# Layer 0's attention in batches of 3, 3 and 2 steps, with bounds sums as accumulator outputs

## The chip, the cores and the metric

The kernel runs on one core of a Trainium2 chip. A core has TensorE (matrix products, PE in the profile, with its weight loads as PEld), VectorE (DVE), ScalarE (ACT), GpSimd (POOL), and DMA queues, of which SyncE (SP) issues most here. The engines run side by side and wait for each other through semaphores. Matrix products land in PSUM, eight banks of 128 rows of 512 fp32 values each; everything else lies in SBUF. The metric is the time of one execution on the device in microseconds (us), the median of several.

## The reference

Eight images of 512 channels and 32x32 = 1024 positions pass through four layers. The change lies in layer 0, attention with 8 heads of 64 channels, and in a check of its own that the kernel makes.

```python
h = group_norm(x, gn_scale, gn_bias)
qkv = einsum('oc,bchw->bohw', qkv_w, h) + qkv_b
q, k, v = split(qkv, 3, axis=1)          # then split into 8 heads of 64
attn = softmax(einsum('bnsd,bntd->bnst', q, k) * 64 ** -0.5, axis=-1)
h = einsum('bnst,bntd->bnsd', attn, v)
for _ in range(3):                       # on h as (positions, channels)
    h = h + 0.1 * tanh(h @ inl_w.T + inl_b)
return x + einsum('oc,bchw->bohw', proj_w, h) + proj_b
# layer 1: attention with one head of 64; layer 2: up-sampling, leaky ReLU,
# down-sampling; layer 3: three convolutions with mixed expert weights
```

## The kernel before

P is 128, S 1024, HALF 512, C 512, CC = C/P = 4, SC = S/P = 8, HD 64, B 8. All values are fp32. Exponentials are taken without subtracting a maximum. So that this is safe, the kernel keeps running sums of all exponential totals and their inverses in `seen`, and at the end counts how many of them are within a bound (1e20); where one is not, the whole computation is done again with a maximum subtracted. With the given inputs this second run is not taken.

The pools that matter: `ps_sc` has two buffers of two PSUM banks, `ps_tp` two of one bank, `ps_mm` two of one bank.

```python
def tmp(name, n=HALF):
    if n == HALF:
        return work.tile([P, n], F32, tag="half", name=name, bufs=2)
    return work.tile([P, n], F32, tag="tmp", name=name, bufs=5)

def sums(name):
    return work.tile([P, S], F32, tag="sums", name=name, bufs=2)
```

Attention of one image is done in 8 groups: a pair of heads (`oc`) and a half of the positions (`sh`). A group has 8 steps (`jc`), one for each 128 keys. A step computes scores for both heads of the pair, which use 64 rows of TensorE each and run side by side, then the exponential, a running sum over steps, and the product with the values. At a group's end the sums over the 128 rows are formed by a product with ones (`total`), inverted and multiplied in.

```python
groups = [(oc, sh) for sh in range(2) for oc in range(CC)]
exps, accs, avs = {}, {}, {}

def scores(t):
    g, jc = divmod(t, SC)
    oc, sh = groups[g]
    ps = ps_sc.tile([P, S], F32, tag="scores", name=f"scores_{b}_{t}")
    scores_T(                                     # two matmuls, L266
        [ps[:, ts(r, HALF)] for r in range(2)],
        [k[rows[r], oc, ts(jc, P)] for r in range(2)],
        [q[rows[r], oc, ts(sh, HALF)] for r in range(2)],
        # ... (shifts, only in the second run)
    )
    e = tmp(f"e_{b}_{t}", S)
    nc.scalar.activation(e, ps, AF.Exp, scale=HD ** -0.5)            # L612
    exps[t] = e
    if jc == 1:
        accs[g] = sums(f"acc_{b}_{g}")
        nc.vector.tensor_add(accs[g], exps[t - 1], e)                # L616
    elif jc > 1:
        nc.vector.tensor_add(accs[g], accs[g], e)                    # L618

def weighted(t):
    g, jc = divmod(t, SC)
    oc, sh = groups[g]
    e = exps.pop(t)
    if jc == 0:
        avs[g] = bank(name=f"av_{b}_{g}")                            # ps_mm
    for r in range(2):
        nc.tensor.matmul(                                            # L627
            avs[g][rows[r]], v[:, jc, ts(2 * oc + r, HD)], e[:, ts(r, HALF)],
            start=(jc == 0), stop=(jc == SC - 1),
        )

def normalised(g):
    oc, sh = groups[g]
    acc = accs.pop(g)
    ps = bank(ps_tp, f"total_{b}_{g}")
    for r in range(2):
        nc.tensor.matmul(                                            # L637
            ps[rows[r]], ones[:, 0:HD], acc[:, ts(r, HALF)], start=True, stop=True
        )
    inv = tmp(f"inv_{b}_{g}", HALF)
    nc.vector.reciprocal(inv, ps)                                    # L641
    nc.vector.tensor_mul(hf[:, oc, ts(sh, HALF)], avs.pop(g), inv)   # L642
    for part in (acc[:, 0:HALF], acc[:, HALF:S], inv):
        nc.gpsimd.tensor_add(seen, seen, part)                       # L644

n = len(groups) * SC
for t in range(0, n + 4, 2):
    for u in (t, t + 1):
        if u < n:
            scores(u)
    for u in (t - 2, t - 1):
        if 0 <= u < n:
            weighted(u)
    if t >= SC + 2 and (t - 2) % SC == 0:
        normalised((t - 2) // SC - 1)
```

After attention come three steps with tanh and the projection. Each is a fast matrix product of seven parts over halves of its operands (P1, C11, U2, ...). `quarter_sums` prepares differences of quarters of `hf` on VectorE (L378 to L381; for the first step they are written over `v`). P1 and C11 need only the first half of the positions; C11 adds into the bank of P1 after ScalarE has copied P1 out:

```python
if what == "P1":
    nc.scalar.copy(keep["P1"][u], ps)                                # L514
elif what == "C11":
    tanh(keep["C11"][u], ps, u)                                      # L508
    step(keep["C11"][u], u, 0)                                       # L505
elif what in ("U2", "U3"):
    nc.vector.tensor_add(keep[what][u], ps, keep["P1"][u])
# ...
order = (
    ("P1", "A", "A11", b11), ("C11", "A", "A12", b21), ("U2", "X", "S2", 1),
    # ... the number is the quarter sum that a part needs; the letter its banks
)
```

The check, near the end of the kernel, beside layer 2 of the last image:

```python
def out_of_bounds():
    within = tmp("within")
    nc.vector.tensor_scalar(within, seen, BOUND, None, ALU.is_le)
    count = small.tile([P, 1], F32, tag="count", name="count")
    nc.vector.tensor_reduce(count, within, AX.X, ALU.add)
    ps = bank(ps_tp, "within")
    nc.tensor.matmul(ps[0:1, 0:1], count, ones[:, 0:1], start=True, stop=True)
    # ... compared with P * HALF - 0.5, read into a register
```

The instructions' order on an engine is not always that of the source: the framework orders them when it builds the program, and adds the waits.

Of the kernel before, what the change touches and what calls it, by code (L numbers as in the profile page):

```python
# [9 lines left out]
F32 = mybir.dt.float32  # L10
BF16 = mybir.dt.bfloat16
AF = mybir.ActivationFunctionType
ALU = mybir.AluOpType
AX = mybir.AxisListType
# [3 lines left out]
P = 128  # L18
B, C, H, W = 8, 512, 32, 32
S = H * W  # L20
CC = C // P
SC = S // P
HALF = 512
NH = 8
HD = C // NH
# [16 lines left out]
BOUND = 1e20  # L42
# [11 lines left out]
def tile_sequence(ctx: ExitStack, tc: tile.TileContext, a: dict, out: bass.AP, shifted: bool):  # L54
    nc = tc.nc
    run = "s" if shifted else "u"

    const = ctx.enter_context(tc.tile_pool(name=f"const_{run}", bufs=1))
    big = ctx.enter_context(tc.tile_pool(name=f"big_{run}", bufs=7))
    work = ctx.enter_context(tc.tile_pool(name=f"work_{run}", bufs=2))  # L60
    small = ctx.enter_context(tc.tile_pool(name=f"small_{run}", bufs=4))
    spill = ctx.enter_context(tc.tile_pool(name=f"spill_{run}", bufs=1, space=DRAM))
    ps_sc = ctx.enter_context(tc.tile_pool(name=f"ps_sc_{run}", bufs=2, space=PSUM))
    ps_tp = ctx.enter_context(tc.tile_pool(name=f"ps_tp_{run}", bufs=2, space=PSUM))
# [5 lines left out]
    def bank(pool=None, name="mm"):  # L70
        pool = pool or ps_mm
        return pool.tile([P, HALF], F32, tag="bank", name=name)

    def tmp(name, n=HALF):
        if n == HALF:
            return work.tile([P, n], F32, tag="half", name=name, bufs=2)
        return work.tile([P, n], F32, tag="tmp", name=name, bufs=5)

    def sums(name):
        return work.tile([P, S], F32, tag="sums", name=name, bufs=2)  # L80
# [28 lines left out]

    seen = const.tile([P, HALF], F32, name="seen")  # L110
    nc.vector.memset(seen, 0.0)

    v_row = const.tile([P, C], F32, name="v_row")
    nc.gpsimd.dma_start(v_row, a["v_b"].partition_broadcast(P))
# [191 lines left out]
    def group_norm(b, x, mul, add):  # L306
        h = big_tile(f"h_{b}", [P, CC, S])
        for cc in range(CC):
            nc.vector.tensor_scalar(
                h[:, cc, :], x[:, cc, :], mul[:, cc : cc + 1], add[:, cc : cc + 1],  # L310
                ALU.mult, ALU.add,
            )
        return h
# [39 lines left out]
    def weight_sums(key, t, a21, a22, held=None):  # L353
        if held is not None:

            nc.gpsimd.tensor_copy(t[:, 3, 0, 0:1], held)
        nc.gpsimd.tensor_add(t[:, 3], a21, a22)
        nc.gpsimd.tensor_sub(t[:, 4], t[:, 3], t[:, 0])
        nc.gpsimd.tensor_sub(t[:, 5], t[:, 0], a21)
        nc.gpsimd.tensor_sub(t[:, 6], t[:, 1], t[:, 4])  # L360
        nc.gpsimd.tensor_scalar(t[:, 2], a22, -1.0, None, ALU.mult)
        nc.gpsimd.dma_start(stored[key], t)
        return t
# [202 lines left out]
    def layer0(b, x, norm, w):  # L566
        h = group_norm(b, x, *norm)
        t = quarter_sums(f"h_{b}", h)
        if b == 0:
            for key in "kv":  # L570
                w[key] = weight_sums(key, *held[key], t[3][1][:, 0:1])
        q = big_tile(f"q_{b}", [P, CC, S])
        k = big_tile(f"k_{b}", [P, CC, S])
        v = big_tile(f"v_{b}", [P, SC, C])
        all_of(product(f"q_{b}", w["q"], h, t, channels(f"q_{b}", q, qkv_b[:, 0:CC])))
        w["inl"] = weight("inl", b)
        all_of(product(f"k_{b}", w["k"], h, t, channels(f"k_{b}", k, qkv_b[:, CC : 2 * CC])))
        w["proj"] = weight("proj", b)
        all_of(product(f"v_{b}", w["v"], h, t, positions(f"v_{b}", v, v_row), rows=True))
        w["v1"] = weight("v1", b)  # L580
        hf = big_tile(f"hf_{b}", [P, CC, S])
        rows = [slice(HD * r, HD * r + HD) for r in range(2)]
        shifts = None
        if shifted:
            shifts = big_tile(f"shifts_{b}", [P, CC, S])
            for oc in range(CC):
                for r in range(2):
                    row_shifts(
                        f"{b}_{oc}_{r}", [q[rows[r], oc, :]] * 2,
                        [k[rows[r], oc, ts(h, HALF)] for h in range(2)],  # L590
                        [shifts[HD * r : HD * r + 1, oc, :]],
                    )

        groups = [(oc, sh) for sh in range(2) for oc in range(CC)]
        exps, accs, avs = {}, {}, {}

        def scores(t):
            g, jc = divmod(t, SC)  # L600
            oc, sh = groups[g]
            ps = ps_sc.tile([P, S], F32, tag="scores", name=f"scores_{b}_{t}")
            scores_T(
                [ps[:, ts(r, HALF)] for r in range(2)],
                [k[rows[r], oc, ts(jc, P)] for r in range(2)],
                [q[rows[r], oc, ts(sh, HALF)] for r in range(2)],
                shifts and [
                    shifts[HD * r : HD * r + 1, oc, ts(sh, HALF)] for r in range(2)
                ],
            )  # L610
            e = tmp(f"e_{b}_{t}", S)
            nc.scalar.activation(e, ps, AF.Exp, scale=HD ** -0.5)  # L612
            exps[t] = e
            if jc == 1:
                accs[g] = sums(f"acc_{b}_{g}")
                nc.vector.tensor_add(accs[g], exps[t - 1], e)  # L616
            elif jc > 1:
                nc.vector.tensor_add(accs[g], accs[g], e)  # L618

        def weighted(t):  # L620
            g, jc = divmod(t, SC)
# [3 lines that stand above are left out]
                avs[g] = bank(name=f"av_{b}_{g}")  # L625
# [14 lines that stand above are left out]
            inv = tmp(f"inv_{b}_{g}", HALF)  # L640
            nc.vector.reciprocal(inv, ps)  # L641
            nc.vector.tensor_mul(hf[:, oc, ts(sh, HALF)], avs.pop(g), inv)  # L642
            for part in (acc[:, 0:HALF], acc[:, HALF:S], inv):
                nc.gpsimd.tensor_add(seen, seen, part)  # L644

        n = len(groups) * SC
        for t in range(0, n + 4, 2):
            for u in (t, t + 1):
                if u < n:
                    scores(u)  # L650
            for u in (t - 2, t - 1):
                if 0 <= u < n:
                    weighted(u)
            if t >= SC + 2 and (t - 2) % SC == 0:
                normalised((t - 2) // SC - 1)

        for it in range(3):
            t = quarter_sums(f"hf_{b}_{it}", hf, None if it else v)
            name = f"inl_{b}_{it}"

            banks = None if it else [bank(p, f"{name}_A{u}") for u, p in enumerate((ps_mm, ps_tp))]
            all_of(product(name, w["inl"], hf, t, inner_step(name, hf), first_banks=banks))
        if b + 1 < B:
            w["q"] = weight("q", b + 1)
        t = quarter_sums(f"hf_{b}_3", hf)
        all_of(product(f"proj_{b}", w["proj"], hf, t, residual(f"proj_{b}", x)))
        if b + 1 < B:
            w["k"] = weight("k", b + 1)
# [366 lines left out]
    for i in (1, 2, 3):  # L1035
        g, be, m, v = (load_const(f"{c}{i}", pool3) for c in "gbmv")
# [45 lines left out]
    for i in range(2):  # L1082
        t = pool3.tile([P, H + 2, W + 2], F32, tag=f"rim_{i}", bufs=1, name=f"rim_{i}")
# [17 lines left out]
    def out_of_bounds():  # L1101


        within = tmp("within")
        nc.vector.tensor_scalar(within, seen, BOUND, None, ALU.is_le)
        count = small.tile([P, 1], F32, tag="count", name="count")
        nc.vector.tensor_reduce(count, within, AX.X, ALU.add)
        ps = bank(ps_tp, "within")
        nc.tensor.matmul(ps[0:1, 0:1], count, ones[:, 0:1], start=True, stop=True)
        redo = small.tile([P, 1], mybir.dt.int32, tag="redo", name="redo")  # L1110
        nc.vector.tensor_scalar(redo[0:1, :], ps[0:1, 0:1], P * HALF - 0.5, None, ALU.is_lt)
        return nc.values_load(redo[0:1, 0:1], min_val=0, max_val=1)

    z3 = {}
# [13 lines left out]
    redo = None if shifted else out_of_bounds()  # L1128
    wt_next = mixed(0)
    route(B - 1, B)  # L1130
    for b in range(B):
# [5 lines left out]
        for g in range(2):  # L1137
            ps = bank(name=f"c1_{b}_{g}")
# [21 lines left out]
        for oc in range(CC):  # L1160
            at = C + 9 * P + oc * P
            ps = ps_sc.tile([P, S], F32, tag="scores", name=f"c3_{b}_{oc}")
# [5 lines left out]
            n = S if b + 1 < B else HALF  # L1168
# [75 lines left out]
```

## Time and profile before

| What | Value |
|---|---|
| Time, median of 3 runs | 3939.58 us (3938.11 to 3940.49) |
| Profiled span | 3934.4 us |
| Busy: PE, DVE, ACT, POOL | 98%, 66%, 28%, 11% |
| Attention scores, L266 | 2048 matmul instructions, 511.0 us busy |
| Weighted values, L627 | 2048 matmul instructions, 494.1 us busy |
| Exponentials, L612 | 512 instructions of 128x1024, mean 1021 ns |
| One attention group in mid-image | 16.00 us: PE busy 16.00, DVE 12.75, ACT 7.75, POOL 5.55 |

Reading it: an fp32 matmul shows as two instructions, so a step's two products are four instructions in each of L266 and L627. Busy time is the union of an engine's instructions; the mean of one matmul is longer than its share, because neighbours overlap. The chain of the work that ended last follows the span back from its end: at each step to whatever released the instruction, or to the one before it on its engine. Time of an engine that does not stand on this chain costs nothing by itself.

### The profile page before, as it was taken

Reading aid. Unit: us, or ns where it says so; the run is one execution under the profiler, and the core shown is the slowest. Engines: PE = TensorE matmul, PEld = TensorE weight load, DVE = VectorE, ACT = ScalarE, POOL = GpSimd, SP = SyncE. Lnnn points to the kernel's source line nnn. Section 1 sums busy time; section 2 is a strip of 40 time slices with the busy share of each in tenths; the row PEclk is TensorE's granted clock in tenths of the full one; section 3 lists DMA queues with packets and bytes.
Section 4 is the critical chain, followed back from the end, with each engine's and each line's share of the span. In section 5 each row is a group of like instructions: output and inputs, shape, how many; then the busy total and the mean of one; then the engine's idle time right before and its main releaser. Section 6 shows DMA issues by size and latency. Waiting matters only on the chain.

```text
span 3934.4 us, 37957 instructions
## 1 busy us (share of the span) xinstructions
PE 3868.2 (98%) x14630; PEld 2032.6 (52%) x14630; DVE 2593.8 (66%) x3690; ACT 1105.0 (28%) x1507; POOL 436.1 (11%) x310
## 2 busy tenths in 40 slices
PE   8999999999999999999999999999999999999998
PEld 4336653476435763366434754357534764346543
DVE  4777848764686647775586646765487655766786
ACT  1421224212332114212241123322142122421333
POOL 5310003000120003100030002200031001301000
PEclk9999999999999999999999999999999999999999
DMA  5002310122101310023101221013200131003432
GB/s 197 19 0 83 115 57 1 40 77 100 38 0 59 118 68 11 0 83 115 56 1 59 79 81 37 1 70 107 78 1 24 60 115 57 1 0 112 164 134 103
DMA packets 85792, 247.86 MB, mean 63 GB/s; under 512 B 10480, under 2 KB 33024, under 8 KB 78816
## 3 DMA queue, kind: packets, MB, share of 16 engines
q1 hardware_dynamic: 69712, 220.23, 15.8%
q10 hardware_dynamic: 13824, 12.59, 1.0%
q0 software_dynamic: 2064, 12.51, 0.8%
q8 instruction: 117, 1.92, 0.2%
q14 instruction: 75, 0.61, 0.0%
HBM read 185.40 MB, written 59.90 MB: 62 GB/s over the span
## 4 chain that ended last, share of the span: by engine, by line
PE 90%; DVE 7%; issue 1%; DMA 1%; ACT 1%; SPq 0%; DVEq 0%; ACTq 0%
PE scores L266 13%; PE av L627 11%; PE inl_X L414 6%; PE dn L941 6%; PE up L920 5%; PE v_X L414 4%; PE inl_Y L414 4%; PE av_X L854 4%; PE c L1150 3%; PE v_Y L414 3%; PE av_A L854 3%; PE v_A L414 3%; PE inl_A L414 3%; PE av_Y L854 2%; PE proj_X L414 2%; PE q_X L414 2%
## 5 line engine op out<-in xcount | busy, mean ns | idle before, releaser
L612 ACT ACTIVATE e<-scores 128x1024 f32<-128x1024 f32 x512 | 497.1, 1021 | 632.7 <-PE scores L266 632.0
L618 DVE TENSOR_TENSOR acc<-acc,e 128x1024 f32<-128x1024 f32 x384 | 494.1, 1287 | 122.7 <-ACT e L612 101.6
L266 PE MATMUL scores<-q,k 64*128 64x512 f32 x2048 | 511.0, 616 | 7.0 <-ACT e L612 3.6
L627 PE MATMUL av<-e,v 128*64 128x512 f32 x2048 | 494.1, 604 | 0.0
L644 POOL TENSOR_TENSOR seen<-seen,acc 128x512 f32<-128x512 f32 x128 | 212.3, 1659 | 1574.9 <-DVE acc L618 1569.9
L266 PEld LDWEIGHTS scores<-q,k 64*128 64x128 f32 x2048 | 175.7, 186 | 334.3 <-ACT e L612 163.2
L627 PEld LDWEIGHTS av<-e,v 128*64 128x64 f32 x2048 | 124.8, 136 | 338.8 <-issue 335.8
L941 PEld LDWEIGHTS dn<-dn_op,up 128*128 128x128 f32 (+1 forms) x2048 | 239.9, 192 | 46.3 <-issue 24.3
L904 DVE SCALAR_TENSOR_TENSOR up<-up,leak 128x512 f32<-128x512 f32 (+1 forms) x264 | 174.9, 687 | 132.9 <-ACT leak L903 124.9
L941 PE MATMUL dn<-dn_op,up 128*128 128x126 f32 (+5 forms) x2048 | 244.7, 275 | 10.1 <-DVE up L904 9.5
L903 ACT ACTIVATE leak<-up 128x512 f32<-128x512 f32 (+1 forms) x264 | 150.0, 595 | 248.9 <-DVE up L904 125.4
L641 DVE RECIPROCAL inv<-total 128x512 f32<-128x512 f32 x64 | 214.7, 3354 | 0.0
L920 PE MATMUL up<-halo,up_op 126*128 126x512 f32 (+1 forms) x384 | 182.8, 605 | 0.4 <-DVE up L904 0.3
L414 PE MATMUL inl_X<-T_hf,w_inl 128*128 128x512 f32 x384 | 172.6, 592 | 0.0
L644 POOL TENSOR_TENSOR seen<-seen,inv 128x512 f32<-128x512 f32 x64 | 125.1, 1955 | 417.6 <-DVE inv L641 417.6
L414 PE MATMUL inl_A<-hf,w_inl 128*128 128x512 f32 x384 | 169.5, 594 | 0.0
L616 DVE TENSOR_TENSOR acc<-e,e 128x1024 f32<-128x1024 f32 x64 | 85.0, 1329 | 102.4 <-ACT e L612 100.7
L508 ACT ACTIVATE inl_U<-inl_U,inl_b 128x512 f32<-128x512 f32 x96 | 64.0, 714 | 304.7 <-DVE inl_U L523 304.7
L519 DVE TENSOR_TENSOR inl_U<-inl_X,inl_P 128x512 f32<-128x512 f32 x96 | 61.8, 685 | 116.0 <-PE inl_X L414 116.0
L736 POOL TENSOR_TENSOR seen<-seen,acc 128x512 f32<-128x512 f32 x16 | 22.6, 1410 | 1019.9 <-DVE acc L728 1019.9
L1150 PE MATMUL c<-rim,mixed 128*128 128x512 f32 x288 | 124.9, 592 | 0.0
L414 PEld LDWEIGHTS inl_A<-hf,w_inl 128*128 128x128 f32 x384 | 72.3, 190 | 94.5 <-issue 88.8
(302 smaller groups left out, 5757.6 us busy)
## 6 DMA issues: line engine op xcount, KB each, us to landing
halo<-ypad_u SPq DMA_DIRECT2D x128, 252.0 KB
halo<-ypad_u SPq DMA_DIRECT2D x128, 198.0 KB
w_v<-stored_u_v SPq DMA_DIRECT2D x14, 1792.0 KB
x<-in_x_dram SPq DMA_DIRECT2D x32, 512.0 KB
spill_u<-z SPq DMA_DIRECT2D x28, 512.0 KB
z<-spill_u SPq DMA_DIRECT2D x28, 512.0 KB
out_dram<-z SPq DMA_DIRECT2D x28, 512.0 KB
w_q<-stored_u_q SPq DMA_DIRECT2D x7, 1792.0 KB
```

Source lines behind the costliest of these rows:

```text
L266: nc.tensor.matmul(ps[r], k[r], q[r], start=True, stop=(shift is None))
L414: nc.tensor.matmul(dst, lhs, rhs, start=(opens and s == 0 and cc == 0), stop=(cc == 1 and s == rows), skip_group_check=True,)
L612: nc.scalar.activation(e, ps, AF.Exp, scale=HD ** -0.5)
L618: nc.vector.tensor_add(accs[g], accs[g], e)
L627: nc.tensor.matmul(avs[g][rows[r]], v[:, jc, ts(2 * oc + r, HD)], e[:, ts(r, HALF)], start=(jc == 0), stop=(jc == SC - 1),)
L641: nc.vector.reciprocal(inv, ps)
L644: nc.gpsimd.tensor_add(seen, seen, part)
L854: nc.tensor.matmul(ps[:, ts(s, QR)], left[:, j, at : at + P], right[:, j, :], start=(what in ("P1", "U2", "W") and s == 0 and j == 0), sto ...
L904: nc.vector.scalar_tensor_tensor(dst, ps, SQRT2, t, ALU.mult, ALU.max)
L920: nc.tensor.matmul(ps[i], op[0 : IR * n, :], halo.tile(t)[0 : IR * n, c + i, :], start=True, stop=True,)
L941: nc.tensor.matmul(rows[:, r0 - first : r1 + 1 - first, c0 : c1 + 1], up[t][0:k, c, ts(cc, P)], op[:, r0 - 4 * t + 3 : r1 + 4 - 4 * t, c0 ...
L1150: nc.tensor.matmul(banks[g].rearrange("p (h w) -> p h w", w=W), wt[:, at : at + P], h1[:, ky + 16 * g : ky + 16 * g + 16, kx : kx + W], st ...
```

## The change

It takes attention's steps in batches of 3, 3 and 2 within each group, in place of batches of 2, so that TensorE changes less often between scores and weighted values. The third step of a batch (steps 2 and 5) gets its scores in two single banks of `ps_tp`, since `ps_sc` holds only two steps; its exponential is two instructions. A sixth buffer for the exponentials goes with it. The totals of a group stand behind the first batch of the next group's weighted values. GpSimd's running sums of layer 0 are replaced: the last addition of a group gives a sum per row as an accumulator output, and a Copy on ScalarE gives the same for the inverses; both go into a small table `seen_sums`, which the check at the end counts too.

```diff
-        return work.tile([P, n], F32, tag="tmp", name=name, bufs=5)
+        return work.tile([P, n], F32, tag="tmp", name=name, bufs=6)
...
+    NG = 2 * CC
+    seen_sums = const.tile([P, B, 2 * NG], F32, name="seen_sums")
+    nc.vector.memset(seen_sums, 0.0)
...
-            ps = ps_sc.tile([P, S], F32, tag="scores", name=f"scores_{b}_{t}")
+            apart = jc in (2, 5)
+            if apart:
+                ps = [bank(ps_tp, f"scores_{b}_{t}_{r}") for r in range(2)]
+            else:
+                pair = ps_sc.tile([P, S], F32, tag="scores", name=f"scores_{b}_{t}")
+                ps = [pair[:, ts(r, HALF)] for r in range(2)]
...
-            nc.scalar.activation(e, ps, AF.Exp, scale=HD ** -0.5)
+            if apart:
+                for r in range(2):
+                    nc.scalar.activation(e[:, ts(r, HALF)], ps[r], AF.Exp, scale=HD ** -0.5)
+            else:
+                nc.scalar.activation(e, pair, AF.Exp, scale=HD ** -0.5)
...
-            elif jc > 1:
+            elif 1 < jc < SC - 1:
                 nc.vector.tensor_add(accs[g], accs[g], e)
+            elif jc == SC - 1:
+                nc.vector.scalar_tensor_tensor(
+                    accs[g], accs[g], 1.0, e, ALU.mult, ALU.add,
+                    accum_out=seen_sums[:, b, g : g + 1],
+                )
...
-            for part in (acc[:, 0:HALF], acc[:, HALF:S], inv):
-                nc.gpsimd.tensor_add(seen, seen, part)
-        # (the loop over t in twos, shown above)
+            copies[g] = inv
+
+        def copied(g):
+            inv = copies.pop(g)
+            nc.scalar.activation(
+                inv, inv, AF.Copy, accum_out=seen_sums[:, b, NG + g : NG + g + 1]
+            )
+
+        batches = [
+            range(g * SC + i, g * SC + j)
+            for g in range(len(groups)) for i, j in ((0, 3), (3, 6), (6, 8))
+        ]
+        for i in range(len(batches) + 1):
+            for t in batches[i] if i < len(batches) else ():
+                scores(t)
+            for t in batches[i - 1] if i else ():
+                weighted(t)
+
+            g, part = divmod(i, 3)
+            if g and (part == 1 or i == len(batches)):
+                normalised(g - 1)
+            if g and (part == 2 or i == len(batches)):
+                copied(g - 1)
...
+        columns = seen_sums.rearrange("p b g -> p (b g)")
+        nc.vector.tensor_scalar(columns, columns, BOUND, None, ALU.is_le)
+        count0 = small.tile([P, 1], F32, tag="count0", name="count0")
+        nc.vector.tensor_reduce(count0, columns, AX.X, ALU.add)
+        nc.vector.tensor_add(count, count, count0)
...
-        nc.vector.tensor_scalar(redo[0:1, :], ps[0:1, 0:1], P * HALF - 0.5, None, ALU.is_lt)
+        nc.vector.tensor_scalar(redo[0:1, :], ps[0:1, 0:1], P * (HALF + B * 2 * NG) - 0.5, None, ALU.is_lt)
```

More of the change, by code (lines that the diff above doesn't have):

```diff
@@ L596, in layer0 @@
         groups = [(oc, sh) for sh in range(2) for oc in range(CC)]
-        exps, accs, avs = {}, {}, {}
+        exps, accs, avs, copies = {}, {}, {}, {}
         def scores(t):
@@ L601, in scores @@
             oc, sh = groups[g]
-            ps = ps_sc.tile([P, S], F32, tag="scores", name=f"scores_{b}_{t}")
+            apart = jc in (2, 5)
[4 more added lines that the diff above has]
+                ps = [pair[:, ts(r, HALF)] for r in range(2)]
             scores_T(
-                [ps[:, ts(r, HALF)] for r in range(2)],
+                ps,
                 [k[rows[r], oc, ts(jc, P)] for r in range(2)],
@@ L642, in normalised @@
             nc.vector.tensor_mul(hf[:, oc, ts(sh, HALF)], avs.pop(g), inv)
-            for part in (acc[:, 0:HALF], acc[:, HALF:S], inv):
[L644 to L655, printed above, removed]
+            copies[g] = inv
[18 more added lines that the diff above has]
+                copied(g - 1)
         for it in range(3):
```

## The prediction

> **What bounds the kernel now.** I began with the page's first two parts, busy time by engine and the 40 slices, to learn whether one engine carries the whole span.
>
> ```profile
> PE 3868.2 (98%) x14630; PEld 2032.6 (52%) x14630; DVE 2593.8 (66%) x3690; ACT 1105.0 (28%) x1507; POOL 436.1 (11%) x310
> PEclk9999999999999999999999999999999999999999
> ```
>
> TensorE is busy 98% of the time at full granted clock. Only 3934.4 - 3868.2 = 66 us are visibly idle, so a gain must come from making TensorE's work shorter, or from those 66 us. The page's chain of the work that ended last says where its work lies:
>
> ```profile
> PE 90%; DVE 7%; issue 1%; DMA 1%; ACT 1%; SPq 0%; DVEq 0%; ACTq 0%
> ```
>
> The two lines changed most, the scores (L266) and the weighted values (L627), lead the chain's list with 13% and 11%. To see what one unit costs there I asked for the chain in order of time over two groups of image 0 (start, length, what):
>
> ```profile
> 117.01 1.92 PE scores L266 x8
> 118.93 1.87 PE av L627 x8
> 120.80 1.92 PE scores L266 x8
> ...
> 130.28 1.87 PE av L627 x8
> 132.15 0.86 PE total L637 x4
> 133.01 1.92 PE scores L266 x8
> ```
>
> A group takes 133.01 - 117.01 = 16.00 us and holds no wait: four batches, each of two steps of scores and two of weighted values, and one total. Is a batch's price proportional to its steps? The end of an image answers, where two weighted batches follow each other without scores between. From the timeline of image 2's end (start, length, instructions; idle time before, and its releaser, in brackets):
>
> ```profile
> 1137.41 1.94 PE L627 MATMUL av<-e,v 128*64 128x512 f32 x8
> ...
> 1141.19 3.65 PE L627 MATMUL av<-e,v 128*64 128x512 f32 x16
> 1141.50 4.36 DVE L618 TENSOR_TENSOR acc<-acc,e 128x1024 f32<-128x1024 f32 x3
> 1145.78 0.69 DVE L380 TENSOR_TENSOR v<-hf 128x512 f32<-128x512 f32 x1
> 1145.92 1.08 PE L637 MATMUL total<-acc,ones 128*64 128x512 f32 x4 [1.07 <-DVE acc L618]
> ...
> 1149.74 3.35 DVE L641 RECIPROCAL inv<-total 128x512 f32<-128x512 f32 x1
> ...
> 1155.10 2.84 PE L414 MATMUL inl_X<-v,w_inl 128*128 128x512 f32 x6 [0.18 <-DVE v L379]
> ```
>
> Two more steps cost 3.65 - 1.94 = 1.71 us, 0.857 a step, although a batch alone occupies 1.87. So each batch of weighted values carries 1.87 - 1.71 = 0.16 that belongs to the change of kind, and each of scores 1.92 - 1.71 = 0.21: 0.37 per pair of batches. Check against the group: 16 x 0.857 + 0.86 + 4 x 0.365 = 16.03, measured 16.00. The row also shows what differs: scores have 64 rows and 128 columns (64*128), weighted values and totals 128*64. The same view shows two waits at an image's end, 1.07 us for the last addition and 0.18 in the next product.
>
> Last, the groups by line, for VectorE and GpSimd:
>
> ```profile
> L618 DVE TENSOR_TENSOR acc<-acc,e 128x1024 f32<-128x1024 f32 x384 | 494.1, 1287 | 122.7 <-ACT e L612 101.6
> L644 POOL TENSOR_TENSOR seen<-seen,acc 128x512 f32<-128x512 f32 x128 | 212.3, 1659 | 1574.9 <-DVE acc L618 1569.9
> L641 DVE RECIPROCAL inv<-total 128x512 f32<-128x512 f32 x64 | 214.7, 3354 | 0.0
> L644 POOL TENSOR_TENSOR seen<-seen,inv 128x512 f32<-128x512 f32 x64 | 125.1, 1955 | 417.6 <-DVE inv L641 417.6
> ```
>
> GpSimd's 337 us of running sums are off the chain (nothing on TensorE waits for L644), but the additions beside them take up to 2.11 us where free ones take 1.16.
>
> [...] the table loads in front of L612 are 8, one an image, though copies (L514) and Tanh (L508) run between. [...] L505, 128x512 from SBUF, takes 684 ns, as L642's plain multiply does (679). With accumulator no run shows it yet.
>
> **The change, part by part.**
>
> 1. Batches of 3, 3, 2 in place of 2, 2, 2, 2. The steps stay: same matmuls. Pairs of changes per group go from 4 to 3, on the path. Saved: 8 groups x 8 images x 0.36 = 23 us. A group should take 16.00 - 0.36 = 15.64 us.
>
> 2. Three steps at a time need a third PSUM place; steps 2 and 5 use two single banks, and their exponentials are two instructions of 128x512 instead of one of 128x1024. L716, the same kind, takes 601 ns, so 2 x 0.60 in place of 1.02: ScalarE has 6 x 1.02 + 4 x 0.60 = 8.5 us a group of 15.6. It is beside TensorE: step 3 reuses the bank of step 0 after three scores and two weighted steps (4.7 us later), with the exponential done some 2.2 us after the start. No wait there.
>
> 3. Those banks are shared with the total, so step 2 of the next group needs the reciprocal done. The total ends 11.0 us into a group (2.78 + 1.87 + 2.78 + 2.72 + 0.86); the reciprocal, 3.35, ends at 14.5, and step 2 of the next group starts at 15.6 + 1.9 = 17.5. Margin 3 us, no wait.
>
> 4. Start of each image. The third step can run before the first exponential. Images 1 to 7 show a 0.30 us wait for L612 at step 3, which goes: 7 x 0.3 = 2.1. Image 0 idles 0.91 us at 97.10 with only two steps done; three steps done, less a short wait for exponential 2, leaves about 0.7. Together 3 us.
>
> 5. GpSimd's three sums per group leave; VectorE's additions drop to about 1.16 to 1.23. Seven are about 8.5 us, then reciprocal 3.35, multiply 0.68 and some 0.15 for reading the accumulator: 12.7 of 15.6. Still not the bound. In the middle of an image this is worth nothing. At its end it is: after total 6, VectorE now does the reciprocal, four additions and the multiply, one slowed. Then it does 3.35 + 0.68 + 2 x 1.2 = 6.4 us, while TensorE does 1.92 + 2.72 + 1.71 = 6.35. So the 1.07 wait shrinks to 0.2: 8 x 0.87 = 7 us. Behind the total, the subtractions L379 and L381 (1.76 and 1.64 beside GpSimd's sums) should fall to about 0.7, so reciprocal 7 starts 2 us earlier and the 0.18 wait and its neighbour of about 0.06 go: 8 x 0.24 = 2 us.
>
> 6. Added: one Copy per group on ScalarE with an accumulator, 0.6 to 0.8 us, 9.3 of 15.6 us there, off the path if it is placed behind the exponentials of its batch. A sixth buffer loosens, adds no work. One memset and three small instructions in the bounds check, about 0.15 us each by the other small ones there (L1054, L1063): below 1 us, on VectorE beside the last downsampling, of which I charge 0.3.
>
> Sum: 23 + 3 + 7 + 2 - 0.3 = 35 us, 3939.6 - 35 = 3905 us.
>
> **The rivals.**
>
> - A: the ends are not improved. The order on VectorE is not that of the source: the trace has an addition between reciprocal and multiply (1139.83), and two L378 subtractions between additions. If the order puts more ahead of the last addition, [...] the wait stays about 1 us. Then 23 + 3 + 1 = 27: 3913 us.
> - B: the Copy blocks ScalarE at the image's end. If it stands ahead of the copies of inl_P (L514), it waits for reciprocal 7, and C11's matmuls, which add into the same bank, wait for that copy. With the reciprocal ending 3.4 us after the total and P1's matmuls after 3.4 us, that costs 1 to 4 us an image, 8 to 30 in all: 3913 to 3935. Against it: ready instructions are evidently taken first (the L380 to L381 subtractions precede the reciprocal at 1149.74).
> - C: shared banks make scores wait for the reciprocal, if VectorE runs 3 us late. Then each group gives back up to its 0.36: 3928 or more. VectorE's 80% load speaks against it.
> - D: the sixth buffer also frees the products outside attention, which use the same tiles. Their visible waits are small: of the 66 idle us about 33 are the kernel's start, 20 are points 4 and 5. At most 5 us more: 3900.
>
> **Range and chances.** Point 1 is nearly fixed, since it is read from two independent places; points 4 and 5 give or take 8 us, and a new order elsewhere another 5. 3893 to 3919 should hold it 8 times in 10. 2% would be 79 us, more than all idle time and twice point 1: 0.02 for faster; slower by 2% needs 1.2 us per group of new waiting: 0.01.
>
> **What would show it.** In the chain of the changed kernel: scores x12 of about 2.78 and av x12 of about 2.72, groups 15.64 apart, no VectorE or ScalarE between groups. Scores before the first weighted step without a wait for L612. At the image's end a total with under 0.4 us of waiting. Additions with a mean near 1.2. If groups are still 16.0 apart, the price is per step or instruction and point 1 is wrong; if the reciprocal stands in front of scores, C; if inl_A waits for inl_P's copy, B.

## The result, and the profile after

| Kernel | Median, us | Lowest to highest | Ratio to before, 95% interval |
|---|---|---|---|
| before | 3940.03 | 3938.11 to 3940.97 | |
| changed | 3907.77 | 3907.65 to 3909.81 | 0.992 (0.9903 to 0.9937) |

The changed kernel is 32.3 us faster. 3905 us were predicted, 2.8 us less than measured, with a range of 3893 to 3919.

The page of the changed kernel, engines first:

```profile
PE 3848.7 (98%) x14630; PEld 2047.3 (52%) x14630; DVE 2545.6 (65%) x3758; ACT 1149.7 (29%) x1763; POOL 99.1 (3%) x118
...
PE 92%; DVE 5%; DMA 1%; issue 1%; ACT 1%; SPq 0%; ACTq 0%; DVEq 0%
```

TensorE has the same 14630 matmuls and is busy for 19.5 us less. The chain in order of time shows where, in the middle of image 0:

```profile
120.53 1.92 PE scores L270 x8
122.45 2.73 PE av L645 x12
125.18 2.78 PE scores L270 x12
127.95 1.87 PE av L645 x8
129.82 2.78 PE scores L270 x12
132.60 2.73 PE av L645 x12
135.32 0.86 PE total L655 x4
136.18 1.92 PE scores L270 x8
```

Batches of three steps are 2.78 and 2.73 us long, and a group 136.18 - 120.53 = 15.65 us. No other engine stands between them: the reciprocal and the exponentials keep up.

The timeline of image 2, at its start and at its end, shows what did not come out as predicted. First the start in the kernel before (ScalarE, then TensorE):

```profile
994.16 1.28 ACT L612 ACT_TABLE_LOAD   x1 [17.97 <-DVE k L451]
1017.92 1.02 ACT L612 ACTIVATE e<-scores 128x1024 f32<-128x1024 f32 x1 [22.47 <-PE scores L266]
...
1016.74 1.13 PE L266 MATMUL scores<-q,k 64*128 64x512 f32 x4
...
1021.64 1.94 PE L627 MATMUL av<-e,v 128*64 128x512 f32 x8
```

Then start and end in the changed kernel:

```profile
1009.91 1.13 PE L270 MATMUL scores<-q,k 64*128 64x512 f32 x4
...
1011.12 1.28 ACT L625 ACT_TABLE_LOAD   x1 [41.76 <-PE scores L270]
...
1011.45 5.05 PE L270 MATMUL scores<-q,k 64*128 64x512 f32 x20 [0.41 <-DVE v L499]
...
1012.41 1.94 ACT L625 ACTIVATE e<-scores 128x1024 f32<-128x1024 f32 x2
...
1016.44 2.79 PE L645 MATMUL av<-e,v 128*64 128x512 f32 x12
...
1127.73 1.03 PE L655 MATMUL total<-acc,ones 128*64 128x512 f32 x4
...
1128.42 1.29 DVE L382 TENSOR_TENSOR v<-hf 128x512 f32<-128x512 f32 x2
...
1128.69 1.99 PE L270 MATMUL scores<-q,k 64*128 64x512 f32 x8
...
1129.63 3.35 DVE L659 RECIPROCAL inv<-total 128x512 f32<-128x512 f32 x1
...
1135.85 1.08 PE L655 MATMUL total<-acc,ones 128*64 128x512 f32 x4 [0.73 <-DVE acc L633]
...
1143.83 3.60 PE L418 MATMUL inl_X<-v,w_inl 128*128 128x512 f32 x8
```

At the start the table of Exp (ACT_TABLE_LOAD, an instruction of 1.28 us on ScalarE) is now loaded only after the first scores, while TensorE already runs; the first exponential starts 2.50 us after the first scores, where it was 1.18 before (1016.74 to 1017.92 in the same image). In the kernel before, images 0 and 1 already had the load there; in the changed kernel all eight have it. At the end the two subtractions L382 stand between total 6 and its reciprocal, and the last total still waits 0.73 us. The product inl_X behind it no longer waits.

From such timelines the stages can be added up, from the first matmul of one to that of the next. Attention took 1042.8 us before and 1015.7 after, 27.2 less; the tanh steps behind it 581.2 and 577.7, 3.5 less. Together that is 30.7 us. In the one profiled run of each kernel all other stages came out 4.3 us longer after, of which 1.8 are told of at the very end of this document; the medians of all runs differ by 32.3.

### The profile page after: what moved, and what is told of

Read it like the earlier page. It is cut to its first block, busy times and chain, and to the rows that moved or that the text cites. A ratio compares the mean times of both kernels' runs of the same rounds, so it can differ in the third digit from the quotient of the medians.

```text
span 3908.0 us, 37846 instructions
## 1 busy us (share of the span) xinstructions
PE 3848.7 (98%) x14630; PEld 2047.3 (52%) x14630; DVE 2545.6 (65%) x3758; ACT 1149.7 (29%) x1763; POOL 99.1 (3%) x118
## 3 DMA queue, kind: packets, MB, share of 16 engines
q8 instruction: 117, 1.92, 0.2%
## 4 chain that ended last, share of the span: by engine, by line
PE 92%; DVE 5%; DMA 1%; issue 1%; ACT 1%; SPq 0%; ACTq 0%; DVEq 0%
PE scores L270 13%; PE av L645 10%; PE inl_X L418 6%; PE dn L970 6%; PE up L949 4%; PE v_X L418 4%; PE inl_A L418 4%; PE inl_Y L418 4%; PE av_X L883 3%; PE c L1184 3%; PE v_Y L418 3%; PE av_A L883 3%; PE v_A L418 3%; PE av_Y L883 2%; PE q_X L418 2%; PE proj_X L418 2%
## 5 line engine op out<-in xcount | busy, mean ns | idle before, releaser
L270 PE MATMUL scores<-q,k 64*128 64x512 f32 x2048 | 495.0, 610 | 3.8 <-DVE v L499 3.3
L645 PE MATMUL av<-e,v 128*64 128x512 f32 x2048 | 480.0, 601 | 0.0
L625 ACT ACTIVATE e<-scores 128x1024 f32<-128x1024 f32 x384 | 372.8, 1023 | 325.7 <-PE scores L270 325.5
L631 DVE TENSOR_TENSOR acc<-acc,e 128x1024 f32<-128x1024 f32 x320 | 389.3, 1217 | 89.9 <-ACT e L625 67.9
L629 DVE TENSOR_TENSOR acc<-e,e 128x1024 f32<-128x1024 f32 x64 | 79.3, 1239 | 122.2 <-ACT e L625 122.2
L623 ACT ACTIVATE e<-scores 128x512 f32<-128x512 f32 x256 | 140.6, 615 | 0.0
L883 PE MATMUL av_X<-v,eT 128*128 128x256 f32 x512 | 120.5, 383 | 1.8 <-DVE av_W L862 1.0
L418 PEld LDWEIGHTS inl_X<-T_hf,w_inl 128*128 128x128 f32 x384 | 72.4, 190 | 92.4 <-issue 72.7
```

The costliest lines, as they stand in the source:

```text
L270: nc.tensor.matmul(ps[r], k[r], q[r], start=True, stop=(shift is None))
L418: nc.tensor.matmul(dst, lhs, rhs, start=(opens and s == 0 and cc == 0), stop=(cc == 1 and s == rows), skip_group_check=True,)
L625: nc.scalar.activation(e, pair, AF.Exp, scale=HD ** -0.5)
L645: nc.tensor.matmul(avs[g][rows[r]], v[:, jc, ts(2 * oc + r, HD)], e[:, ts(r, HALF)], start=(jc == 0), stop=(jc == SC - 1),)
L883: nc.tensor.matmul(ps[:, ts(s, QR)], left[:, j, at : at + P], right[:, j, :], start=(what in ("P1", "U2", "W") and s == 0 and j == 0), sto ...
```

## The experiments

The theory is the prediction's: a fixed price of 0.36 us for each pair of changes between scores and weighted values. The main rival is that the gain came from taking the sums off GpSimd, which frees VectorE. Smaller terms have rivals of their own. Times are medians, and ratios are to the kernel before, which was run beside each set on the same chip, with medians of 3937.7 us (e1 to e4), 3938.7 (e5, e7, e8, e9) and 3938.8 (e6, e10, e11). The changed kernel was not run again beside them; where it differs from an experiment by a few us only, the stages in the traces are the better measure.

**e1_twos: the batches undone.**

```diff
-            apart = jc in (2, 5)
+            apart = False
 # and the loop over t in twos of the kernel before; copied(g) one batch behind normalised(g)
```

> Batches of 2 again, everything else as in the changed kernel (sums as accumulator outputs, sixth buffer). Theory (a price of 0.36 us for each pair of changes between scores and weighted values): one more pair per group, 64 groups, so 23 us are given back and about 3931 us are measured, groups 16.0 us apart. Rival (the gain comes from taking GpSimd's sums off, which frees VectorE): it stays near 3908 to 3912, groups 15.65 apart or little more.

Measured: 3940.8 us, ratio 1.0005 (0.9996 to 1.0014). From the chain of waits:

```profile
1041.00 1.92 PE scores L270 x8
...
1056.14 0.86 PE total L655 x4
1057.00 1.92 PE scores L270 x8
```

Groups are 16.00 us apart again, with the sums still off GpSimd: the rival falls. But 33 us were given back and not 23. An image's attention takes 130.89 us against 126.95 in the changed kernel, 3.94 more. Eight pairs of changes are 8 x 0.35 = 2.8. The timeline of image 2 shows the rest: the first weighted step comes after 5.55 us and four steps, in the changed kernel after 6.53 and six, and two steps are 1.71 us, so the start costs 0.73 more. Step 2 is what waits there:

```profile
1021.10 2.04 PE L270 MATMUL scores<-q,k 64*128 64x512 f32 x8 [0.91 <-ACT e L625]
```

The third place in PSUM let TensorE work through the table load; without it the load is exposed. At the end a Copy stands ahead of an exponential; weighted values wait 0.23 us for that, and the last total 0.60. So the sums as accumulator outputs, with a sixth buffer but without the batches, gain nothing measurable over the kernel before. That is a balance of two things: by the stages, the tanh steps are 3.5 us shorter than in the kernel before, and attention is 4.4 us longer, 4.0 of them because the table load is exposed in six more images (5.55 us to the first weighted step in place of 4.90).

**e2_batches_only: the sums undone.** The batches and the sixth buffer stay.

```diff
-            elif jc == SC - 1:
-                nc.vector.scalar_tensor_tensor(... accum_out=...)
-            copies[g] = inv     # and copied(g)
+            for part in (acc[:, 0:HALF], acc[:, HALF:S], inv):
+                nc.gpsimd.tensor_add(seen, seen, part)
```

> Batches of 3, 3 and 2, but the running sums on GpSimd as before. Theory: groups 15.65 apart all the same; only an image's end is worse, by the 0.34 us more of waiting for the last total and 0.45 us in the stretch behind it, 8 images, 6 us: about 3914 us. Rival (sums are the cause): near 3932 or above.

Measured: 3914.7 us, ratio 0.9931 (0.9914 to 0.9947). Groups are 15.64 us apart (133.61 - 117.97 in its chain). The end of image 2 and the additions, from its timeline and its groups by line:

```profile
1135.55 1.08 PE L650 MATMUL total<-acc,ones 128*64 128x512 f32 x4 [1.19 <-DVE acc L631]
...
1136.02 1.75 DVE L383 TENSOR_TENSOR v<-hf,v 128x512 f32<-128x512 f32 x1
...
1144.73 2.84 PE L418 MATMUL inl_X<-v,w_inl 128*128 128x512 f32 x6 [0.18 <-DVE v L383]
```

```profile
L631 DVE TENSOR_TENSOR acc<-acc,e 128x1024 f32<-128x1024 f32 x384 | 536.3, 1397 | 39.4 <-ACT e L625 11.9 <-DVE acc L631 0.5 <-ACT e L623 0.5
```

Both waits of the kernel before are back, and a subtraction beside GpSimd's sums takes 1.75 us again, where it takes 0.69 in the changed kernel. The additions have a mean of 1397 ns here, more than before (1287) and in the changed kernel (1217), and still a group is no longer. Batches alone gain 23 us, and the sums on top of them 7: by the stages 3.7 in attention, where the last addition of an image takes 1.70 us here and 1.22 and 0.08 in the changed kernel, and 3.5 in the tanh steps. The slowing beside GpSimd's sums is real, 1397 ns against 1217, but it counts only at an image's end.

**e3_across: batches of 3 throughout.**

```diff
-            apart = jc in (2, 5)
+            apart = t % 3 == 2
+        batches = [range(i, min(i + 3, n)) for i in range(0, n, 3)]
 # total and reciprocal behind the batch of weighted values with step 1 of the next group
```

> Batches of 3 steps throughout, across the borders of groups: 22 batches an image in place of 24. Theory: two pairs of changes fewer per image, 2 x 0.36 x 8 = 5.7 us faster than the changed kernel, about 3902 us. Rival (the gain comes from the slack of deeper batches within a group and is used up): no difference, 3908, or a new wait where the total and the single banks meet.

Measured: 3983.9 us, ratio 1.0114 (1.0097 to 1.0131); the expectation missed by 82 us. The chain of waits:

```profile
1051.62 0.88 PE total L655 x4
...
1052.53 3.37 DVE inv L659
...
1055.94 1.12 PE scores L270 x2
```

This is the prediction's rival C, not in the change but in its neighbour. Now every batch needs both single banks, the total holds one until its reciprocal has read it, and the third step of the very next batch wants it. The batch of two at a group's end is thus not a remainder: it has no third step, and so gives the reciprocal its time.

**e4_total_inside: one more pair of changes, nothing else.**

```diff
+            g, part = divmod(i, 3)
             for t in batches[i] if i < len(batches) else ():
                 scores(t)
+                if g and part == 2 and t == batches[i][0]:
+                    normalised(g - 1)
```

> The changed kernel with the total of a group put between the two scores steps of the next group's last batch, in place of behind weighted values, in 7 of 8 groups. Same instructions, same batches, one more pair of changes in 56 groups. Theory (price per change): 56 x 0.36 = 20 us slower, about 3928 us. Rival (price per batch or per wait, not per change): no difference, about 3908 us.

Measured: 3923.2 us, ratio 0.9953 (0.9937 to 0.997), 15.5 us above the changed kernel. The chain:

```profile
1037.01 1.06 PE scores L270 x4
1038.07 1.01 PE total L655 x4
1039.08 1.06 PE scores L270 x4
```

1.06 + 1.01 + 1.06 = 3.13 us, against 0.86 + 1.92 = 2.78 for the same twelve instructions in the changed kernel: 0.35 us for one pair of changes, with no wait, no other batch and no other instruction. Groups are 16.00 us apart. That is 19.6 us over 56 groups; some 5 came back at the images' ends, where two matmuls of inl_A moved ahead of the last total and filled its wait. The price is per change: that is now shown. Here it is a change of shape that counts, 64*128 to 128*64, and not one of product: a total behind weighted values, both 128*64, takes 0.86 us for four instructions, just what four more of the weighted values cost.

**e8_early and e7_early_apart14: the start of an image.**

```diff
+        first_exp = small.tile([P, 1], F32, tag="first_exp", name=f"first_exp_{b}", bufs=1)
+        nc.scalar.activation(first_exp, k[:, 0, 0:1], AF.Exp)
 # e7 also:
-            apart = jc in (2, 5)
+            apart = jc in (1, 4)
```

> The changed kernel with one exponential of a 128x1 column of k before the attention of each image, so that the table of Exp is loaded while ScalarE is idle. The start of an image in the changed kernel has 0.77 us more than 6 steps, one change and the 0.41 us wait for v explain. Theory (the table load stands behind the wait for the first scores and delays the first exponential by 1.28 us, and step 3 waits for it): 0.77 x 8 = 6 us faster, about 3902 us. Rival (the start is bound by v's last values on VectorE): no difference, 3908 us.

> The same early table, and single banks for steps 1 and 4 in place of 2 and 5, so that step 1 needn't wait 0.41 us for VectorE to empty the second pair of banks. Theory: 0.41 x 8 = 3.3 us faster than with the early table alone, about 3898 us. Rival: the wait moves to step 2, no difference from the early table alone.

Measured: 3905.3 us (0.9909, 0.9893 to 0.9926) and 3895.9 us (0.9888, 0.9871 to 0.9904). The early table gains 2.4 us by the medians, and 0.50 us an image, 4.0 in all, by the stages, less than the 6 expected. By the timeline the first weighted step comes 6.03 us after the first scores in place of 6.53, so 0.5 us of the 0.77 counted went, and 0.27 stayed beside the 0.41 for VectorE. With both the start has no wait left, as e7's timeline shows:

```profile
1007.49 5.42 PE L270 MATMUL scores<-q,k 64*128 64x512 f32 x24
...
1012.84 2.79 PE L647 MATMUL av<-e,v 128*64 128x512 f32 x12
```

Six steps in a row, 5.35 us to the first weighted one, in place of 6.53. An image's attention takes 125.58 us in place of 126.95.

**e6_apart14: single banks for steps 1 and 4, without the early table.**

> The changed kernel with the single banks for steps 1 and 4 in place of 2 and 5, and no early table. Theory (step 3 waits for the first exponential, which waits for the table, so that starting step 1 earlier only lengthens that wait): 0 to 1 us faster, 3907 us. Rival (the 0.41 us at step 1 count by themselves): 3.3 us faster, 3904 to 3905 us.

Measured: 3907.5 us, 0.992 (0.9904 to 0.9937). The timeline of image 2:

```profile
1015.08 3.02 PE L270 MATMUL scores<-q,k 64*128 64x512 f32 x12 [0.73 <-ACT e L625]
```

The wait for VectorE at step 1 is gone, step 3 waits 0.73 us for an exponential, and the first weighted step comes after 6.53 us, as in the changed kernel. As expected, taking away one of two waits in a row only makes the other longer. At an image's start the early table alone is worth 0.50 us, the other banks alone nothing, both together 1.18. (Attention is 0.19 us an image shorter all the same: the last total waits 0.54 us in place of 0.73. With the start's 1.18 that makes e7's 1.37.)

**e11_bufs5: the sixth buffer undone.**

```diff
-        return work.tile([P, n], F32, tag="tmp", name=name, bufs=6)
+        return work.tile([P, n], F32, tag="tmp", name=name, bufs=5)
```

> The changed kernel with five buffers for the exponentials, as before. Theory (the sixth buffer is not what gains): the exponential of a third step waits for the first weighted step of its batch, but nothing on TensorE waits for it; 3908 us, within 4. Rival (batches of 3 live on the sixth buffer): a wait of some tenths in each group, 3920 us or more.

Measured: 3901.7 us (3900.4 to 3902.9), 0.9904 (0.9888 to 0.9921): 6 us faster, just outside the 4 allowed. Attention is 0.69 us shorter in images 2 to 7 (0.49 at the start, 0.20 at the last total) and 0.2 to 0.3 in the first two. The table loads in front of the exponentials, by groups of lines (the idle time before them, and what ended it), in the changed kernel and then with five buffers:

```profile
L625 ACT ACT_TABLE_LOAD x8 | 10.3, 1283 | 334.2 <-PE scores L270 334.2
```

```profile
L625 ACT ACT_TABLE_LOAD x8 | 10.3, 1283 | 191.3 <-DVE k L455 107.8 <-PE scores L270 83.5
```

With six buffers all eight loads wait for scores; with five, as in the kernel before, six of the eight run after `k`, long before the scores. The kernels e1 to e6, all with six buffers, have all eight behind the first scores too, whatever their batches and sums. The sixth buffer is thus not only not needed but moves the load onto the start of the image. That it does so by changing what the first exponential has to wait for is likely, but only argued: the runs show where the load stands, not why. The 4.6 us of attention explain most of the 6; the rest is within what runs of one kernel differ by.

**e5_across_total_first, e9_all and e10_third_behind_total: batches of 3 throughout, once more.**

```diff
+            for g in ended:
+                total(g)                    # between the scores and the weighted values
             for t in batches[i - 1] if i else ():
                 weighted(t)
 # e5: the second step of each batch has the single banks; e9: and the early table
-            apart = t % 3 == 1 and t < SC * len(groups) - 1
 # e10:
+            behind_total = any(t // 3 == (o * SC + 7) // 3 + 2 for o in range(len(groups)))
+            apart = t % 3 == (2 if behind_total else 1)
```

> Batches of 3 throughout, but the total stands between the scores and the weighted values of its batch, and the single banks serve the second step of a batch, so that the reciprocal has the weighted values and one step (about 3.9 us) before the bank is needed. Theory (batches of 3 across groups lost only by the wait for the reciprocal at the shared bank): no 3.4 us wait per group; two pairs of changes fewer, 5.7 us, and the wait for the last total (0.73 us an image) falls away, since the last batch holds one step: about 3896 us. Rival (crossing the groups' borders costs by itself, in exponentials or additions that come late): well above 3908 us.

> Batches of 3 throughout with the total ahead of the weighted values, and the early table of Exp (step 1 already has its single banks). Theory: the three add up: 5.7 + 5.8 + 6.2 + 3.3 = 21 us below the changed kernel, about 3887 us. If the single terms hold but do not add, 3890 to 3896 us.

> As e9_all, but in the batch behind a total the third step has the single banks, in place of the second. In e5 that batch took 3.66 us in place of 2.78, because the reciprocal began 0.85 us after the total, behind an addition, and held the bank. Theory (all that crossing the groups costs is this wait, 0.88 us in 56 batches): 49 us below e9_all, about 3881 us, and every batch of scores 2.78 us long. Rival (late exponentials behind the Copy on ScalarE, which stands among them, take over): 3900 us or more.

Measured: e5 3938.6 us (1.0002, 0.9993 to 1.0011), e9 3930.2 (0.9978, 0.9969 to 0.9986), e10 3889.4 (0.9871, 0.9855 to 0.9888). The first two missed by 43 us each, the third by 8. Chains of e5, behind the first and the third total of image 2, and of e10, behind the first:

```profile
1034.72 1.01 PE total L655 x4
1035.73 2.58 PE av L645 x12
1038.31 3.66 PE scores L270 x12
...
1069.33 3.35 PE scores L270 x12
```

```profile
1020.82 1.01 PE total L658 x4
...
1024.40 2.80 PE scores L270 x12
```

In e5 an addition that started at 1035.44 held VectorE until the reciprocal could begin at 1036.58, 0.85 us after the total; it ended at 1039.93, after the second step wanted its bank. So an addition did come late, as the rival of e5 had it, but it cost time only through the reciprocal and the bank. With the third step in the second's place the wait is gone (2.80 us). An image's attention fell by 5.4 us from e9 to e10. There are seven batches behind a total in an image, 56 in all as written, but they did not all lose 0.88 us: five took 3.66 us, and the two behind the third and the sixth total 3.35. 5 x 0.86 + 2 x 0.57 = 5.4 us an image, 43 in all, where 49 were expected; the medians differ by 41. The Copy among the exponentials, the rival there, costs nothing that shows. e10 is the fastest kernel of this study: 49 us under the kernel before in its own set, 18 under the changed kernel.

## Why the prediction was right

1. Batches: 23 us predicted, groups of 15.64; measured 15.65, and e1 and e4 give 0.35 us for a pair of changes. Right.

2. Two exponentials in place of one, off the path. Right: no group of the changed kernel waits for ScalarE.

3. The shared bank, margin 3 us, no wait. Right: in the middle of image 2 a reciprocal ends at 1053.93 us, and the third step of the next group starts at about 1057.0 (two steps after its scores begin at 1055.10). e3 and e5 show what the same bank costs where the reciprocal has less time (rival C): in e3 the reciprocal's 3.37 us stand in the chain, in e5 the batch behind a total takes 3.66 us in place of 2.78.

4. Start of an image: 3 us predicted. Image 0 gave 0.7 as said. Image 1 gave as much: it too waited 0.91 us in the kernel before, and not the 0.30 that the prediction read for images 1 to 7. Images 2 to 7 gave 0.08 each, not 0.3: before, the first weighted step came 4.90 us after the first scores, with four steps done; after, 6.53 us with six, and 4.90 + 1.71 - 6.53 = 0.08. This term was mis-sized because the prediction kept the table load where it was. It moved, with the sixth buffer (e11). In all the starts gave about 1.8 us.

5. End of an image: 7 us for the last total, 2 us behind it. The last total's wait fell from 1.07 to 0.73 us, 2.7 us in all, not to 0.2. The step that failed is "Then it does 3.35 + 0.68 + 2 x 1.2 = 6.4 us, while TensorE does 1.92 + 2.72 + 1.71 = 6.35". The work itself was sized rightly, 6.16 us from 1129.63 to 1135.79, but the sum lets it begin when total 6 ends. The two L382 subtractions come first, and the reciprocal begins 0.94 us after the total's end (1128.69), a part of what rival A had named. In the kernel before it began as late, 1.07 us after the total's end, behind an addition and a subtraction, so its trace could have told. Behind the total 0.45 us an image were gained, 3.5 in all, more than the 2 predicted. The prediction took the waits that the view shows, 0.18 and 0.06 us; but from the first inl_X product to the first inl_Y it is 3.43 us after and was 3.87 before. That GpSimd's sums are the cause e2 shows: with them back, the tanh steps take 581.2 us again.

6. Added work. The accumulator form was as fast as a plain addition but for 83 ns to read the accumulator, by the groups of the changed kernel, VectorE's and then ScalarE's:

```profile
L629 DVE TENSOR_TENSOR acc<-e,e 128x1024 f32<-128x1024 f32 x64 | 79.3, 1239 | 122.2 <-ACT e L625 122.2
...
L633 DVE SCALAR_TENSOR_TENSOR acc<-acc,e 128x1024 f32<-128x1024 f32 x64 | 77.9, 1217 | 0.9
...
L633 DVE DVE_READ_ACCUMULATOR acc<-acc,e 128x1 f32 x64 | 5.3, 83 | 0.0
```

```profile
L665 ACT ACTIVATE inv<-inv 128x512 f32<-128x512 f32 x64 | 40.3, 630 | 126.4 <-DVE hf L660 126.4
...
L665 ACT ACTIVATION_READ_ACCUMULATOR inv<-inv 128x1 f32 x64 | 11.9, 186 | 0.0
```

1217 ns and 83 for the accumulator, against 1239 for a plain addition. The Copy is 0.63 + 0.19 us, as estimated, and brings no table load in front of the exponentials: they stay eight. Rival B did not occur: P1's copies (L518) precede the last Copy at every image's end. Nor did rival D: the sixth buffer gained nothing outside attention that shows, and lost time in it. Its count of the idle time was off as well: in the kernel before, the first 36 us hold 16.8 us in which TensorE is idle, where about 33 were counted, and the waits of points 4 and 5 come to 3.6 + 8.6 + 1.4 = 13.6 us, where 20 were.

The sum by stages: 64 x 0.35 = 22.4 for the groups, 1.8 for the starts, 2.7 for the last totals, 26.9 of the 27.2 that attention lost; 3.5 behind it. 30.7 us against 35 predicted: the terms of the starts and of the last totals were too high, that of the stretch behind them too low. That the total came out within 2.8 us is in part luck: these errors offset each other in part, and the medians differ by 1.6 us more than the stages explain.

## What to carry to other kernels

Where products of two tile shapes alternate, count the changes of shape in the chain and price one by comparing runs of different length, here 0.35 us a pair; then batch, as far as PSUM has places. A place that is shared with a slow reader (a 3.4 us reciprocal) needs as much work between as the reader takes, or a shorter batch there. Of two waits in a row measure both away together, and after each change look again at where table loads and small instructions have come to stand.

## What the runs showed of the hardware that was not expected

The kernel's start lost 1.8 us in the profiled run of the changed kernel, in a stretch whose code did not change. The window from 30 to 32 us (busy time with counts of TensorE, its weight loads, VectorE, ScalarE and GpSimd; granted clock; share and GB/s of the DMA engines), first before, then after:

```profile
30.00:32.00 2.00, 2.00 (x6) 0.84 (x5) 0.24 (x1) 0.00 (x0) 1.97 (x3) 1.00 0.97 416
```

```profile
30.00:32.00 2.00, 2.00 (x3) 0.66 (x2) 0.14 (x1) 0.00 (x0) 1.79 (x3) 0.50 1.07 452
```

Half the clock, three matmuls in place of six, after TensorE had waited 1.87 and 1.68 us for VectorE (before: 1.11 and 1.69, and full clock). In the changed kernel's trace the clock is 0.50 from 29.4 to 32.8 us and 1.00 on either side. With five buffers the waits were 1.19 and 0.62 us, and the clock was full.

The length of a wait does not tell the cases apart by much: e10 waited 1.78 and 1.68 us and fell to half (the six matmuls of q_X behind the second wait take 4.54 us, where they take 2.84 in the kernel before), e5 waited 1.77 and 1.69 and did not. That is read from one execution of each kernel. What decided whether the clock fell was not tested by an experiment, and these traces do not show it.
